# The steps of a recurrence, nine to a channel block, cut into ten (eight in the first token block)

## The chip, the cores and the metric

One core of one Trainium2 chip. Its engines work side by side, each through its own queue in order: PE (matrix products), DVE (elementwise work, scans), ACT (activation functions, copies), POOL (elementwise work), SP (here it only issues DMAs). The metric is the device time of one launch in microseconds (us); lower is better.

## The reference, cut to what matters

x is 4 sequences of 2048 tokens of 512 channels, in f32. The output is x plus two branches of its layer norm xn:

```
r, k, v = mixes of xn and the token before, times Wr, Wk, Wv        # 512 channels
per channel, from token to token (aa, bb, pp carried; decay w, bonus u):
    p  = max(pp, u + k);    e1  = exp(pp - p);      e2  = exp(u + k - p)
    y  = (e1 aa + e2 v) / (e1 bb + e2)
    p2 = max(pp + w, k);    e1b = exp(pp + w - p2); e2b = exp(k - p2)
    aa, bb, pp = e1b aa + e2b v,  e1b bb + e2b,  p2
branch 1 = (sigmoid(r) * y) Wo
hidden   = fwht(silu(xn W1) * (xn W3))                              # 2048 channels
branch 2 = hidden W2
```

The recurrence over tokens (wkv in the code) is what the change is about.

## The kernel before, in words

The tokens are worked through in eight blocks of 1024 (the loop `for i in range(n_blocks)`, i from 0), two to a sequence. Channels lie on the 128 partitions, so the 512 channels of r, k and v are four channel blocks of 128, h = 0 to 3. Each token block has these stages:

- **Projections** to r, k and v. Block 0 does them as plain products. Every later block does them as six **pairs**, n = 0 to 5 (`projected_pair`): pairs 0 and 1 give k, 2 and 3 give v, 4 and 5 give r. Pair n gives the rows of two channel blocks, h = 0 and 2 for even n, 1 and 3 for odd n. In front of the pairs stands up tile 0.
- **Up tiles**, j = 0 to 15 (`up`): the two products of the gated branch for 128 hidden channels each, gated with a tanh. 
- **Down**: the products with the two output matrices (the Hadamard transform is folded into W2 in block 0), the residual, the stores. Beside them run the token statistics, and in part the normalization, of later blocks.

A pair or an up tile is one run of `seven`, a Strassen-like scheme with seven products where eight would be plain. Its order on PE, with what other engines must have done before the next product, is this:

```
        product(pa, 0, m11, True)
        act.copy(pb, pa)
        product(pf, 4, f1, True)
        act.copy(s5, pf)
        product(pb, 5, f2, False)
        act.copy(pc, pb)
        for f in tail:
            f()
        product(pa, 1, m21, False)
        on11(pa)
        product(pb, 3, f3, False)
        act.copy(pd, pb)
        on22(pa, pb, s5)
        product(pc, 6, m22, False)
        on12(pc, s5)
        product(pd, 2, f4, False)
```

Each product adds onto a PSUM bank that ACT has just copied from another, so PE waits for such a copy, and ACT does its queue in order. f1 to f4 are differences of the right side's quarters, made by DVE. The five banks come from a ring of eight: a tile's first product takes the bank that held pb two tiles before. on11, on22 and on12 are the places where a tile's own ACT and DVE work is issued (tanh, sums with s5); `tail` is what the tile before still has to do (in an up tile: the second tanh, and three products on DVE).

**The slots.** The wkv work for a token block is a generator, and each `next` of it issues one **step**, on the queues of DVE and ACT. In up tiles a step is taken in on22 (behind the first gate, ahead of the sum onto pb) and one in on12 (behind the sum onto pc): two slots a tile. In the pairs there are three hooks a pair (on11, on22, on12), numbered 1 to 18, and a list says at which of them a step is taken: 5, 6, 8, 11, 12, 13, 14, 15, 17. The other hooks, and these too, carry the mixing of the inputs for v and r (`mix_chores`): a scaled copy on ACT, a multiply-add on DVE, then the four differences f1 to f4 on DVE. What is left of the generator after the last up tile is issued at once, by `before()`, ahead of down.

The work of one channel block, with the names that the prediction uses for its parts (tiles: sa is a0 and a1, sb is b0 and b1):

- S1: DVE scan for the running maximum into a1, and the first difference, into b1
- S2: DVE second difference, into e1
- S3: ACT two relus, of b1 into e1b and into b1
- S4: ACT two exps, of e1b and b1
- S5: ACT two relus, of e1 into k and into e1; DVE product with v and scan (aa)
- S6: ACT two exps, of k and e1; DVE scan (bb)
- S7: DVE three products and sums, to numerator part and denominator
- S8: DVE reciprocal of the first half of the denominator
- S9: DVE reciprocal of the second half; two steps of the numerator
- S10: DVE two multiply steps into r

The kernel before takes these in nine steps: S1; S3 with S2 behind it; S4; S5; S6; S7; S8; the second reciprocal; the numerator and S10. Block 0 has 4 x 9 = 36 steps and 32 slots; later blocks have 36 steps and 9 + 30 slots. For token blocks 2 to 6 the steps with the relus and with the exps of h = 1 to 3 also carry `ahead`: one and two products of the early normalization of the next block (DVE, slots in pieces_w, loaded and stored by SP).

POOL makes the differences of weights, in token blocks 0 and 1 only. SP loads the weights of an up tile or pair two tiles ahead, into a ring of three.

Down takes its right side from the up tiles and from r. It begins with four runs of ten products on quarters of the right side (the second and fourth on those with the last up tiles and with r of h = 2 and 3), while DVE makes the first differences; the fifth run of ten reads the first difference, which lies in k_sb. All of DVE's work for it is queued behind the last up tile's tail.

Of the kernel before, what the change touches and what calls it, by code (L numbers as in the profile page):

```python
# [11 lines left out]
ALU = mybir.AluOpType  # L12
# [4 lines left out]
H = 512  # L17
TB = 2 * H
# [22 lines left out]
def tile_rwkv_attn_hadamard_ffn(  # L41
# [17 lines left out]
    NB = C // P  # L59
# [7 lines left out]
    pe, dve, act, pool, sp = (InOrder(tc, e) for e in (nc.tensor, nc.vector, nc.scalar, nc.gpsimd, nc.sync))  # L67
# [24 lines left out]
    e1b, e1 = (const.tile([P, TB], F32, name=n) for n in ("e1b", "e1"))  # L92
# [11 lines left out]
    def row_of(kind, h):  # L104
        return r_of(h) if kind == 0 else (k_sb, v_sb)[kind - 1][:, h, :]
# [131 lines left out]
    def first_statistics(half):  # L237
        return token_statistics(f"f{half}", x_first[:, half * HT : (half + 1) * HT, :])

    def first_diagonals(half, rs):  # L240
        diag = v_sb[:, half, :].rearrange("p (s t q) -> p s t q", s=2, q=P)
        for t in range(HT):
            dve.tensor_scalar(diag[:, 0, t], eye_sb, rs[:, 0, t : t + 1], None, ALU.mult)
            act.activation(diag[:, 1, t], eye_sb, AF.Copy, scale=rs[:, 1, t : t + 1])
        return diag

    def first_spread(diag):
        pts = banks[6:8]
        for s in range(2):
            pe.matmul(pts[s], lhsT=ones, rhs=diag[:, s].rearrange("p t q -> p (t q)"), start=True, stop=True)  # L250
        return pts
# [43 lines left out]
    def mixed(kind):  # L295
        for b in range(NB):
            mixed_block(kind, b)


    def load_square(i, kind):  # L300
        t = half_ring({1: 0, 2: 1, 0: 0}[kind], NB, C)
        sp.dma_start(out=t, in_=wrkv[kind])
        return t
# [11 lines left out]
            act.copy(dst, pt)  # L315


    def wkv(h, ahead):

        w_h, u_h = weff[:, h : h + 1], vec[:, 4, h : h + 1]  # L320
        r, k, v = (row_of(kind, h) for kind in range(3))
        a0, a1, b0, b1 = sa[:, OFF - 1 : OFF - 1 + TB], sa[:, OFF : OFF + TB], sb[:, OFF - 1 : OFF - 1 + TB], sb[:, OFF : OFF + TB]
        first_a, first_b, last_a, last_b = a0[:, 0:1], b0[:, 0:1], a1[:, TB - 1 : TB], b1[:, TB - 1 : TB]
        tt, stt, scan, copy = dve.tensor_tensor, dve.scalar_tensor_tensor, dve.tensor_tensor_scan, dve.tensor_copy
        cy = [carry[:, h, n : n + 1] for n in range(3)]

        def below(out, t, sign):
            act.activation(out, t, AF.Relu, scale=-sign)  # L330

        def exp(t):
            act.activation(t, t, AF.Exp, scale=-1.0)

        copy(first_a, cy[0])
        scan(a1, w_h.to_broadcast([P, TB]), k, first_a, ALU.add, ALU.max)
        stt(b1, a0, w_h, k, ALU.add, ALU.subtract)
        copy(cy[0], last_a)
        yield
        below(e1b, b1, 1.0)  # L340
        below(b1, b1, -1.0)
        stt(e1, k, u_h, a0, ALU.add, ALU.subtract)
        ahead(1)
        yield
        exp(e1b)
        exp(b1)
        ahead(2)
        yield

        below(k, e1, 1.0)  # L350
        below(e1, e1, -1.0)
        copy(first_a, cy[1])
        tt(a1, b1, v, ALU.mult)
        scan(a1, e1b, a1, first_a, ALU.mult, ALU.add)
        copy(cy[1], last_a)
        yield
        exp(k)
        exp(e1)
        copy(first_b, cy[2])
        scan(b1, e1b, b1, first_b, ALU.mult, ALU.add)  # L360
        copy(cy[2], last_b)
        yield
        num, den = e1, e1b
        tt(v, k, v, ALU.mult)
        tt(den, e1, b0, ALU.mult)
        tt(den, den, k, ALU.add)
        yield
        dve.reciprocal(den[:, 0:H], den[:, 0:H])
        yield
        dve.reciprocal(den[:, H:TB], den[:, H:TB])  # L370
        yield
        tt(num, e1, a0, ALU.mult)
        tt(num, num, v, ALU.add)
        stt(r, r, 1.0, num, ALU.add, ALU.mult)
        stt(r, r, 0.5, den, ALU.mult, ALU.mult)
        yield
# [12 lines left out]
    def token_forms(eng):  # L389
        for out, x, y in ((t1, b12, b11), (t2, b22, t1), (t3, b22, b12), (t4, b21, t2)):  # L390
            eng.tensor_tensor(out, x, y, ALU.subtract)
            yield
# [59 lines left out]
    def load_parts(i, n):  # L452
        t = ring_a.tile([P, 7, KH, P], F32, tag="a", name=f"part_{i}_{n}")
        if is_first(i, n):
            sp.dma_start(out=t[:, 0:4], in_=wpart[n])
            forms_in(t)
        else:
            sp.dma_start(out=t, in_=part_w[n])
        return t
# [72 lines left out]
    def fold_products(n, m, pts=None):  # L532

        left = []
        for part in (fold[a][:, ts(k, C)] for a in range(n, m) for k in range(2)):
            pt = pts[len(left)] if pts else bank()
            pe.matmul(pt, lhsT=had_sb, rhs=part, start=True, stop=True)
            left.append((part, pt))
        return left

    def fold_evict(left):
        for part, pt in left:
            act.mul(part, pt, 0.5 / float(F) ** 0.5)
# [515 lines left out]
    for i in range(n_blocks):  # L1059
# [8 lines left out]
        def ahead(n):  # L1068
            for _ in range(n if early else 0):
                next(early, None)  # L1070


        pieces = (None for h in range(NB) for _ in wkv(h, ahead if h else lambda n: None))

        def step():
            next(pieces, None)
# [10 lines left out]
        if i == 0:  # L1087
            for kind, after in ((1, 2), (2, 0), (0, None)):
                w = w_next
                if after is not None:  # L1090
                    w_next = load_square(i, after)
                    if kind != 1:
                        mixed(after)
                if kind == 2:
                    for _ in token_forms(pool):
                        pass
                if kind == 1:
                    got = []

                    def spread_more():  # L1100
                        dve.tensor_scalar(weff, weff, -1.0, None, ALU.mult)
                        got.append(first_spread(first_diagonals(1, first_statistics(1))))

                    def fold_more():
                        got.append(fold_products(3, 4, banks[4:6]))

                    def spread_after():
                        fold_evict(got.pop(0))
                        spread_more()

                    left = first_k(0, w, spread_0, [], fold_more, lambda: None, spread_after)
                    folded_4 = fold_products(4, 5, banks[4:6])
                    left.append(lambda: fold_evict(folded_4))
                    left = first_k(1, w, got[0], left, lambda: None, lambda: None, lambda: mixed(2))
                    for f in left:
                        f()
                    turn[0] = NB
                for n in range(2 * NB if kind != 1 else 0):
                    projected(kind, w, n // 2, n % 2)
                    if kind == 2 and n == 2:  # L1120
                        fold_evict(fold_products(5, NP))
                        folded = fold_butterflies()
            parts = [load_parts(i, n) for n in order_of(i)[:2]]
        else:


            def mix_chores(*kinds):
                for kind in kinds:
                    mix_before(kind, 0)
                    for b in range(NB):  # L1130
                        if b + 1 < NB:
                            mix_before(kind, b + 1)
                        mix_here(kind, b)
                        yield
                    yield from mix_forms(kind)

            for b in range(NB):
                mix_here(1, b)
            k_forms = mix_forms(1)
            tail = up(i, 0, group(0), tail, lambda: next(k_forms))  # L1140
            for _ in k_forms:
                pass
            chores, hooks = mix_chores(2, 0), [0]
            for n in range(3 * KH):

                def hook():
                    hooks[0] += 1
                    for _ in range(1 if hooks[0] % 3 else 2):
                        next(chores, None)
                    if hooks[0] in (5, 6, 8, 11, 12, 13, 14, 15, 17):  # L1150
                        step()

                tail = projected_pair(i, n, group(1 + n), tail, hook)
# [100 lines left out]
```

## Time and profile before

| | us |
|---|---|
| median of three runs (3053.67 to 3057.03) | 3054.59 |
| profiled execution | 3052.48 |
| its span, first to last instruction | 3050.7 |
| PE busy in the span | 3014.0 |
| DVE busy | 2391.1 |
| ACT busy | 1153.9 |
| POOL busy | 213.7 |

The views used are the page (busy shares, the chain that ended last), the chain of waits in order of time (start, duration, engine, tile written), the timeline of an engine (start, duration, engine, line, operation, tiles, shape, count, and in brackets the idle time before and what ended it), and the view of stretches (length, busy time and count of PE, PEld, DVE, ACT, POOL, then the granted PE clock, DMA share, GB/s). All instructions issued through one helper have line 35, so groups are told apart by their tiles. The ends of matmuls are modelled, so the busy share of PE hides short gaps; the distance between the starts of matmuls shows them.

### The profile page before, as it was taken

What the parts mean: (1) busy time and instruction counts of PE and PEld (TensorE: products, weight loads), DVE (VectorE), ACT (ScalarE), POOL (GpSimd) and SP (SyncE); (2) the same over time, 40 slices, a digit from 0 to 9 for tenths busy, and PEclk for the clock granted to TensorE, in tenths of its full rate; (3) what the DMA queues carried; (4) which work ended last, traced back from release to release, by engine and by line L of the source; (5) the groups of instructions that cost most, each with busy time, mean ns of one, the idle gap of its engine ahead of it and who ended that gap; (6) DMA issues with size and microseconds to landing.
All of it is one profiled execution on the core that took longest, in us unless ns stands there. A gap on an engine that the chain in (4) does not pass through costs nothing.

```text
span 3050.7 us, 24995 instructions
## 1 busy us (share of the span) xinstructions
PE 3014.0 (99%) x8702; PEld 1653.5 (54%) x8702; DVE 2391.1 (78%) x2525; ACT 1153.9 (38%) x1992; POOL 213.7 (7%) x196
## 2 busy tenths in 40 slices
PE   8999999999999999999999999999999999999999
PEld 3444444447644486444854448544584445844468
DVE  7687647788878887787877878778787887877777
ACT  4334134433244333543235332443424443153421
POOL 3253012220000000000000000000000000000000
PEclk9999999999999999999999999999999999999999
DMA  4265623666422264222733236332363323622234
GB/s 174 87 209 199 220 86 128 214 215 225 141 107 102 95 228 136 105 102 85 242 122 122 98 115 218 116 121 86 139 206 105 133 86 121 203 99 73 84 128 151
DMA packets 146332, 429.14 MB, mean 141 GB/s; under 512 B 15392, under 2 KB 33824, under 8 KB 144032
## 3 DMA queue, kind: packets, MB, share of 16 engines
q1 hardware_dynamic: 145920, 426.96, 40.8%
q8 instruction: 70, 1.15, 0.2%
q10 hardware_dynamic: 288, 0.59, 0.1%
q14 instruction: 54, 0.44, 0.0%
HBM read 354.76 MB, written 72.74 MB: 140 GB/s over the span
## 4 chain that ended last, share of the span: by engine, by line
PE 95%; DVE 3%; ACT 1%; DMA 1%; issue 0%; POOL 0%; SPq 0%; DVEq 0%; ACTq 0%; POOLq 0%
PE bank L35 95%; DVE sa L35 1%; DVE e1b L35 0%; DVE right L35 0%; DMA pieces_w<-down_w 0%; DVE sb L35 0%; ACT tf L35 0%; ACT bank L35 0%; ACT e1b L35 0%; ACT sb L35 0%; DVE pieces_w L35 0%; DMA right<-w 0%; DVE v_sb L35 0%; DMA part<-wpart 0%; DVE e L35 0%
## 5 line engine op out<-in xcount | busy, mean ns | idle before, releaser
L35 PE MATMUL bank<-tf,part 128*128 128x512 f32 x2048 | 943.7, 593 | 5.0 <-ACT bank L35 5.0
L35 ACT COPY bank<-bank 128x512 f32<-128x512 f32 (+1 forms) x659 | 344.8, 523 | 1195.5 <-PE bank L35 1167.2
L35 PE MATMUL bank<-right,pieces_w 128*128 128x256 f32 (+1 forms) x2928 | 733.5, 409 | 1.6 <-DMA pieces_w<-down_w 1.6
L35 PE MATMUL bank<-xnT,part 128*128 128x512 f32 x1536 | 721.9, 592 | 0.2 <-DVE right L35 0.2
L35 PEld LDWEIGHTS bank<-tf,part 128*128 128x128 f32 x2048 | 389.3, 190 | 496.4 <-issue 456.9
L35 PEld LDWEIGHTS bank<-right,pieces_w 128*128 128x128 f32 x2928 | 556.2, 190 | 167.6 <-issue 99.3
L35 PEld LDWEIGHTS bank<-xnT,part 128*128 128x128 f32 x1536 | 291.9, 190 | 365.6 <-issue 361.9
L35 DVE SCALAR_TENSOR_TENSOR right<-right,bank 128x512 f32<-128x512 f32 x256 | 175.1, 684 | 301.7 <-ACT right L35 301.3
L35 PE MATMUL bank<-right,part 128*128 128x512 f32 x840 | 371.9, 596 | 0.0
L35 DVE TENSOR_TENSOR right<-right 128x1280 f32<-128x1280 f32 (+2 forms) x236 | 328.1, 1416 | 9.5 <-PE bank L35 8.5
L35 PEld LDWEIGHTS bank<-right,part 128*128 128x128 f32 x840 | 159.6, 191 | 205.4 <-issue 188.8
L35 ACT ACTIVATE right<-bank 128x512 f32<-128x512 f32 x308 | 184.5, 600 | 120.8 <-PE bank L35 109.9
L35 DVE RECIPROCAL e1b<-e1b 128x512 f32<-128x512 f32 x64 | 213.8, 3342 | 0.0
L35 DVE TENSOR_TENSOR right<-right,bank 128x512 f32<-128x512 f32 x256 | 173.6, 678 | 13.8 <-PE bank L35 9.4
L35 DVE TENSOR_TENSOR bank<-bank,s 128x512 f32<-128x512 f32 x256 | 167.1, 689 | 21.1 <-ACT bank L35 12.2
L35 DVE SCALAR_TENSOR_TENSOR right<-xnT,vec,right 128x1024 f32<-128x1024 f32 x92 | 121.7, 1353 | 40.6 <-ACT right L35 40.6
L35 PE MATMUL bank<-k_sb,pieces_w 128*128 128x256 f32 x630 | 146.3, 379 | 0.0
L35 PEld LDWEIGHTS bank<-k_sb,pieces_w 128*128 128x128 f32 x630 | 119.7, 190 | 16.3
L35 ACT COPY s<-bank 128x512 f32<-128x512 f32 x128 | 75.0, 586 | 136.3 <-PE bank L35 136.3
L35 PE MATMUL bank<-pieces_w,part 128*128 128x512 f32 x224 | 103.7, 601 | 15.6 <-ACT bank L35 13.3
L35 POOL TENSOR_SCALAR mean<-sums 128x8 f32<-128x8 f32 x7 | 4.8, 682 | 1568.2 <-ACT tf L35 1568.2
L35 ACT ACTIVATE right<-xnT,omm 128x1024 f32<-128x1024 f32 x92 | 100.3, 1141 | 1.9 <-PE bank L35 1.9
(120 smaller groups left out, 2350.1 us busy)
## 6 DMA issues: line engine op xcount, KB each, us to landing
part<-part_w SPq DMA_DIRECT2D x148, 896.0 KB, 4.6
pieces_w<-deep_w SPq DMA_DIRECT2D x343, 320.0 KB, 3.1
part_w<-part SPq DMA_DIRECT2D x22, 896.0 KB, 6.4
pieces_w<-down_w SPq DMA_DIRECT2D x56, 320.0 KB, 4.9
deep_w<-pieces_w SPq DMA_DIRECT2D x7, 2240.0 KB, 10.3
tf<-x SPq DMA_DIRECT2D x7, 2048.0 KB, 8.5
v_sb<-xT SPq DMA_DIRECT2D x48, 256.0 KB, 4.4
out<-v_sb SPq DMA_DIRECT2D x47, 256.0 KB, 2.2
```

The source lines that it names most:

```text
L35: return self.tc.keep_in_program_order(issue(*args, **kwargs))
```

## The change

In token blocks 1 to 7 (`ten` true) a channel block takes ten steps, S1 to S10 each on its own, and hook 9 is added to the list of hooks: ten hooks and thirty slots for forty steps. So the ten steps of a channel block take five tiles of two: S1 and S2, S3 and S4, S5 and S6, S7 and S8, S9 and S10; h = 0 takes its ten in pairs 1 to 5. In token block 0 (`ten` false) there are eight steps in four tiles: S1; S2; S3 and S4 together; S5; S6; S7; S8 with the numerator of S9; the second reciprocal with S10. Instructions are neither added nor removed.

```
-    def wkv(h, ahead):
+    def wkv(h, ahead, ten):
...
         stt(b1, a0, w_h, k, ALU.add, ALU.subtract)
         copy(cy[0], last_a)
         yield
+        stt(e1, k, u_h, a0, ALU.add, ALU.subtract)
+        yield
         below(e1b, b1, 1.0)
         below(b1, b1, -1.0)
-        stt(e1, k, u_h, a0, ALU.add, ALU.subtract)
         ahead(1)
-        yield
+        if ten:
+            yield
         exp(e1b)
         exp(b1)
         ahead(2)
...
         dve.reciprocal(den[:, 0:H], den[:, 0:H])
-        yield
-        dve.reciprocal(den[:, H:TB], den[:, H:TB])
-        yield
+        if ten:
+            yield
+            dve.reciprocal(den[:, H:TB], den[:, H:TB])
         tt(num, e1, a0, ALU.mult)
         tt(num, num, v, ALU.add)
+        yield
+        if not ten:
+            dve.reciprocal(den[:, H:TB], den[:, H:TB])
         stt(r, r, 1.0, num, ALU.add, ALU.mult)
         stt(r, r, 0.5, den, ALU.mult, ALU.mult)
         yield
...
-        pieces = (None for h in range(NB) for _ in wkv(h, ahead if h else lambda n: None))
+        pieces = (None for h in range(NB) for _ in wkv(h, ahead if h else lambda n: None, i > 0))
...
-                    if hooks[0] in (5, 6, 8, 11, 12, 13, 14, 15, 17):
+                    if hooks[0] in (5, 6, 8, 9, 11, 12, 13, 14, 15, 17):
                         step()
```

## The prediction

> **What bounds the kernel now.** I read the page first, then the chain of waits over the whole span, then the timelines of PE, ACT and DVE around each place where the chain leaves PE.
>
> ```profile
> span 3050.7 us, 24995 instructions
> ...
> PE 3014.0 (99%) x8702; PEld 1653.5 (54%) x8702; DVE 2391.1 (78%) x2525; ACT 1153.9 (38%) x1992; POOL 213.7 (7%) x196
> ...
> PE 95%; DVE 3%; ACT 1%; DMA 1%; issue 0%; POOL 0%; SPq 0%; DVEq 0%; ACTq 0%; POOLq 0%
> ```
>
> PE is the bound; DVE is at 78%. So the change, which touches no matmul, can only take or give gaps between matmuls. In the PE timeline a 512-column matmul starts every 0.43 us, a product (four of them) takes 1.72, a tile (seven products) 12.02. Where starts lie further apart, PE waited. I added these excesses up over the span: some 33 us, of which 4 in the first 20 us. The chain shows what most of the others are; here is block 3:
>
> ```profile
> 1217.24 1.29 DVE sb L35
> 1218.56 1.06 ACT e1b L35
> 1219.65 1.06 ACT sb L35
> 1220.71 0.49 ACT bank L35
> 1221.20 0.04 issue
> 1221.25 365.40 PE bank L35 x1090
> ```
>
> Read upwards: PE could run again at 1221.25 because ACT's copy of a bank ended; that copy stood behind two relus, and these waited for the difference b1 (tile sb) from DVE. The first bank copy of the pair (pf done at 1217.15 + 1.72 = 1218.87) was late by **2.38 us**. The chain shows the same five lines in blocks 2 to 7; in block 1 the timeline has it at 465.86 to 468.29 (2.43). Block 1 has it twice more in its up tiles, where POOL slows the scan (3.22 us instead of 2.35): 1.73 at 530.26 and 3.58 at 642.57, with a 0.37 just before it (a bank not read yet).
>
> A gap costs more than itself. The view of stretches, with PEclk behind the busy times:
>
> ```profile
> 1218.95:1222.36 3.41, 1.19 (x4) 0.64 (x4) 3.41 (x4) 2.73 (x4) 0.00 (x0) 1.00 0.12 50
> 1222.37:1225.77 3.40, 3.40 (x6) 1.33 (x5) 0.28 (x1) 1.07 (x2) 0.00 (x0) 0.50 0.00 0
> ...
> 846.91:850.31 3.40, 1.84 (x5) 0.88 (x6) 2.97 (x3) 2.02 (x3) 0.00 (x0) 1.00 0.00 0
> ```
>
> After a stretch of 3.41 us with PE busy 1.19, the next ran at clock 0.50 (matmuls 0.85 us apart): 1.7 us lost. After one with 1.84 busy it did not. Three such half-clock stretches follow gaps of this kind (642.1, 1222.4 and 1969.9).
>
> **The change, part by part.** Steps are named as in the section on the kernel, S1 to S10; h is the channel block.
>
> *The relus get a step of their own, a slot after the second difference.* In pair 1 (block 1 on) hook 6 now issues S2 alone, on DVE, where it stood before; ACT has nothing ahead of the bank copy, so the 2.38 go: 6 x 2.38 + 2.43 = **16.7**. Next late there would be f2 (DVE, done 1214.6) and f3 (done 1220.3, wanted 1222.3): neither is. In the up tiles S3 now always falls in the tile after S1, so b1 is long there: block 1's 1.73 + 3.58 + 0.37 = **5.7** go, and with the gaps the three half-clock stretches, 3 x 1.7 = **5.1**. Given back: 27.5.
>
> *What comes in pair 2.* There S3 (hook 8) and S4 (hook 9) both go to ACT, where before only the exps went. Before, ACT:
>
> ```profile
> 1229.25 0.58 ACT L35 COPY bank<-bank 128x512 f32<-128x512 f32 x1
> 1229.77 1.14 ACT L35 ACTIVATE right<-xnT,omm 128x1024 f32<-128x1024 f32 x1
> 1230.81 1.04 ACT L35 ACTIVATE e1b<-e1b 128x1024 f32<-128x1024 f32 x1
> 1231.76 1.04 ACT L35 ACTIVATE sb<-sb 128x1024 f32<-128x1024 f32 x1
> 1232.71 1.14 ACT L35 ACTIVATE right<-xnT,omm 128x1024 f32<-128x1024 f32 x1
> 1233.75 0.58 ACT L35 COPY bank<-bank 128x512 f32<-128x512 f32 x1
> ```
> ```profile
> 1233.43 3.60 PE L35 MATMUL bank<-pieces_w,part 128*128 128x512 f32 x8
> ```
>
> PE wants the last copy for its fifth matmul of that row, at 1233.43 + 1.72 = 1235.15; it ended at 1234.33. By the starts of such runs (1240.98, 1242.07, 1243.03, 1243.98), relus cost 1.09 and 0.96, exps 0.95 each. New order: mix 1229.77, relus 1230.81 and 1231.90, mix 1232.86, exps 1233.90 and 1234.85, copy 1235.80 to 1236.38, PE at 1236.43: **1.28 late**, in seven blocks 9.0. ACT has made it good by the next copy (the s5 copy has no PE behind it). Its ends: 0 if ACT found room, 2.38 if it cost what the old wait did. The gap leaves PE 2.1 busy in 3.41, more than the 1.84 that kept the clock.
>
> *The last step in the last tile before down.* Before, 36 steps met 39 slots and up tile 15 held none; now 40 meet 40, and it holds S9 and S10 of channel block 3: a reciprocal 3.26, two products 2.40, two into r 2.40: 8.06 of DVE, the rest of that tile unchanged. The queue behind them is the tile's tail, then down's first differences. Before:
>
> ```profile
> 1449.53 0.69 DVE L35 TENSOR_TENSOR right<-right,bank 128x512 f32<-128x512 f32 x1
> 1450.13 1.48 DVE L35 TENSOR_TENSOR k_sb<-right 128x1280 f32<-128x1280 f32 x1
> ```
> ```profile
> 1456.64 2.32 PE L35 MATMUL bank<-k_sb,pieces_w 128*128 128x256 f32 x10
> ```
>
> The difference was ready at 1451.6, PE took it at 1456.64: 5.0 of cover. DVE waited 2.6 us in that tile, which the new work fills: the tile's gated product to 1444.4, reciprocal to 1447.65, products to 1450.05, two bank sums to 1451.25, S10 to 1453.65, tail to 1455.57, difference to 1457.05. PE comes at 1457.12: **0.48 late**, in seven blocks 3.4. Its ends: 0, and 8.06 - 5.0 = 3.0 if none of the waiting is filled. The fourth product of down, which reads r, is wanted at 1454.49; r is done at 1453.7.
>
> *Block 0, eight steps in 16 tiles.* The second tile of a channel block puts S3, S4 and S5's relus on ACT: 1.09 + 0.96 + 0.95 + 0.95 + 1.12 + 0.96 = 6.03 from 133.08, so the copy ends at 139.69 and PE, due at 139.27, comes 0.47 late: four times, **1.9**. The fourth tile gives DVE 4.1 of its own and 2 x 5.7, 15.5 in 12.02. PE cares only when the tile after next takes the bank that the tail's last product reads (the 0.37 above was that). I get 0.6 of room in tile 3, 0.3 late in tile 7, 0.1 of room in tile 11, POOL's slowing counted by the rows there: **0.3**, from 0 to some 4 if all four two-input steps doubled. The four steps that were left for after block 0's last tile (312 to 325) go, but no wait of PE hung on them: the wait at 353.2 is for a transfer queued behind the statistics, and stays.
>
> *Moved at no cost.* The early normalization's products and its SP loads and stores move with S3 and S4 into up tiles 2, 7 and 12; SP's weight loads land in 4.6 us with a tile of room, and pieces_w is wanted again only at tile 15. Without that room a tile would wait up to 4.6. S9's products in pair 4 delay a DVE sum of pair 5 by 0.6, which no matmul reads. Up tiles with S9 and S10 give DVE 11.8 of 12.02; no backlog.
>
> **Sum.** 27.5 - 9.0 - 3.4 - 1.9 - 0.3 = **12.9** less. The profiled execution took 3052.48 (span and 1.8 around it): 3039.6. The runs' median, 3054.59, is 2.1 above it; if the gaps go, so does the half-clock, which I take for part of that spread, so I say **3040** for the median as well.
>
> [...] The trace has half-clock stretches after gaps of 2.4 us. [...]
>
> **Rivals.**
> - *A, pair 2 has room on ACT*: no new wait there, 3039.6 - 9.0 = 3030.6. For: a second of ACT idleness lies behind the copy; against: the copy itself is queued behind the exps. 0.12.
> - *B, the half-clock comes anyway*, from what the rows don't tell: 3039.6 + 5.1 = 3044.7. 0.08.
> - *D, the wait only moves*: pair 2 stalls as long as pair 1 did, 7 x 1.1 = 7.7, and brings two half-clock stretches, 3.4: 3050.7, no change. For: the same ACT queue, the same copy. 0.08.
> - *C, slower: the last channel block isn't done when down begins.* If DVE fills none of its waiting in tile 15, down waits 3.0 instead of 0.48: 7 x 2.5 = 17.6, and gaps of 3.0 bring a half-clock stretch in some four blocks, 6.8: 3064. It outweighs the gain from 2.3 us a block on. Against: the queue walked through above. 0.06.
>
> The forecast itself (3035 to 3043.5) has 0.66. The range 3030 to 3048 holds it with A and B. About 0.2% (6 us) is what a measurement of this kernel can tell from no change: faster 0.86, same 0.08, slower 0.06.
>
> **What would show it.** Right: no relu in the chain at the seven places; ACT's exps ahead of a bank copy in pair 2 and a PE gap of 1.3 behind; clock 1.00 throughout after the start; PE's first k_sb product of down 0.5 late, for a difference; a 0.5 gap in tiles 1, 5, 9 and 13 of block 0. Wrong: gaps over 2 us in pair 2 or at down, a gap at the start of tiles 5, 9 or 13 of block 0, or a half-clock stretch.

## The result, and the profile after

The changed kernel takes 3041.75 us (median of five runs, 3040.17 to 3044.23) against 3056.42 of the kernel before on the same chip: a ratio of 0.9953 (95% interval 0.9938 to 0.9968). The profiled execution took 3040.17, its span 3038.4. The forecast was 3040.

The page of the changed kernel:

```profile
span 3038.4 us, 25004 instructions
...
PE 3010.9 (99%) x8702; PEld 1650.6 (54%) x8702; DVE 2383.3 (78%) x2525; ACT 1152.4 (38%) x1992; POOL 215.1 (7%) x196
...
PE 89%; ACT 3%; DVE 3%; issue 0%; DVEq 0%; ACTq 0%
```

The busy shares tell nothing: 99% and 78% as before. The chain has less PE in it than before (89 for 95%) though the kernel is faster, because it counts the work that it passes through, and between waits that have shrunk to a microsecond it still goes through ACT's and DVE's whole queue. What tells is the distance between the starts of matmuls. In the execution before, PE lost 33 us in gaps of over a quarter microsecond; now 21.5. Some of that is the start, which varies; so in what follows the measure for a trace is the time from the 61st matmul (at some 38 us) to the last: **3008.4 before, 2996.8 after**, 11.5 less.

Where the gaps are now, first pair 2 of block 3 on ACT, then on PE:

```profile
1217.69 1.14 ACT L35 ACTIVATE right<-xnT,omm 128x1024 f32<-128x1024 f32 x1
1218.74 1.04 ACT L35 ACTIVATE e1b<-sb 128x1024 f32<-128x1024 f32 x1
1219.81 1.06 ACT L35 ACTIVATE sb<-sb 128x1024 f32<-128x1024 f32 x1
1220.78 1.13 ACT L35 ACTIVATE right<-xnT,omm 128x1024 f32<-128x1024 f32 x1
1221.82 1.04 ACT L35 ACTIVATE e1b<-e1b 128x1024 f32<-128x1024 f32 x1
1222.76 1.04 ACT L35 ACTIVATE sb<-sb 128x1024 f32<-128x1024 f32 x1
1223.71 0.57 ACT L35 COPY bank<-bank 128x512 f32<-128x512 f32 x1
```
```profile
1221.35 1.88 PE L35 MATMUL bank<-pieces_w,part 128*128 128x512 f32 x4
1224.34 1.98 PE L35 MATMUL bank<-pieces_w,part 128*128 128x512 f32 x4 [1.10 <-ACT bank L35]
```

Mix, two relus, mix, two exps, copy: the queue that the prediction wrote down. PE was due at 1221.35 + 1.72 = 1223.07 and came at 1224.34, 1.27 late. The relus themselves wait for nothing any more, and pair 1 has no gap.

Now the start of down in the same block, ACT and then PE:

```profile
1441.10 0.38 ACT L35 COPY bank<-bank 128x256 f32<-128x256 f32 x1
1443.58 0.69 ACT L35 ACTIVATE bank<-had_sb 128x256 f32<-128x256 f32 x2 [2.11 <-DVE right L35]
1444.21 0.33 ACT L35 COPY bank<-bank 128x256 f32<-128x256 f32 x1
```
```profile
1437.31 6.65 PE L35 MATMUL bank<-right,pieces_w 128*128 128x256 f32 x30
1444.59 2.43 PE L35 MATMUL bank<-right,pieces_w 128*128 128x256 f32 x10 [0.64 <-ACT bank L35]
```

Here the gap is not where it was forecast. Thirty matmuls of 0.216 us end at 1443.79; the fourth run of ten comes 0.80 later, and what it waits for is ACT's copy of 1444.21, which stands behind two clears (the line ahead of it), which waited 2.1 us for DVE.

### The profile page after: what moved, and what is told of

It is laid out like the page before. It is cut to its first block, busy times and chain, and to the rows that moved or that the text cites. A ratio compares the mean times of both kernels' runs of the same rounds, so it can differ in the third digit from the quotient of the medians.

```text
span 3038.4 us, 25004 instructions
## 1 busy us (share of the span) xinstructions
PE 3010.9 (99%) x8702; PEld 1650.6 (54%) x8702; DVE 2383.3 (78%) x2525; ACT 1152.4 (38%) x1992; POOL 215.1 (7%) x196
## 4 chain that ended last, share of the span: by engine, by line
PE 89%; ACT 3%; DVE 3%; issue 0%; DVEq 0%; ACTq 0%
PE bank L35 89%; DVE right L35 1%; ACT right L35 1%; DVE e1b L35 1%; ACT bank L35 1%; ACT sb L35 1%; ACT e1b L35 1%; DVE e L35 1%; DVE bank L35 0%; ACT v_sb L35 0%; ACT k_sb L35 0%; DVE v_sb L35 0%; DVEq L1255 0%; ACT e L35 0%; ACTq L35 0%
```

## The experiments

All are set against the changed kernel. In the traces I give the time from the 61st matmul to the last, which leaves the start out.

**1. The relus back behind b1.** In blocks 1 to 7 only; ten steps and hooks as changed.

```
         stt(b1, a0, w_h, k, ALU.add, ALU.subtract)
         copy(cy[0], last_a)
         yield
+        if ten: below(e1b, b1, 1.0); below(b1, b1, -1.0)
         stt(e1, k, u_h, a0, ALU.add, ALU.subtract)
         yield
-        below(e1b, b1, 1.0); below(b1, b1, -1.0)
+        if not ten: below(e1b, b1, 1.0); below(b1, b1, -1.0)
```

> Ten steps and the hooks as changed, but in token blocks 1 to 7 the relus (S3) go back into the step of the second difference (S2). Theory (the gain comes from taking the relus away from the slot behind b1): the wait of 2.4 us returns in pair 1 of seven blocks, the one of 1.28 in pair 2 goes, block 1's up tiles wait again where POOL slows the scan (1.7 to 4 us in all), and two or three half-clock stretches return (1.7 each). From 3041.75: +16.7 - 9.0 + 3 + 4.3 = 3057, between 3052 and 3060. Rival (the gain comes from ten steps and their even spread over tiles, not from the relus): no change, 3042, and no relu in the chain.

Measured: 3064.99 us (3060.61 to 3068.52); 3022.2 in the trace, 25.4 more than the changed kernel, more than the kernel before too. Pair 1 has its wait in all seven blocks (2.38, and 2.43 in block 1), pair 2 none; block 1's up tiles wait 1.99 and 3.78. The theory holds and the rival falls: ten steps without the move of the relus gain nothing. The size was missed: block 1's two waits came to 5.8, not 3, and above all the half clock came more often than in the two or three stretches expected (4.3): 25.4 - (16.7 - 9.0 + 5.8) = 11.9 us are left for it, some seven times 1.7. The mean granted clock of the profiled run was 0.996, for 1.000 in the changed kernel. The view of stretches shows one with the half clock behind it and, from the same trace, one without (534.65 to 538.05, behind the last line, ran at 1.00):

```profile
1224.14:1227.54 3.40, 1.31 (x4) 0.24 (x2) 3.40 (x5) 2.52 (x3) 0.00 (x0) 1.00 0.44 186
1227.55:1230.95 3.40, 3.28 (x4) 1.51 (x5) 1.53 (x2) 0.58 (x2) 0.00 (x0) 0.50 0.00 0
531.24:534.64 3.40, 1.58 (x5) 0.67 (x4) 2.62 (x4) 2.69 (x4) 3.40 (x2) 1.00 0.24 98
```

**2. The exps one hook later.**

```
-                    if hooks[0] in (5, 6, 8, 9, 11, 12, 13, 14, 15, 17):
+                    if hooks[0] in (5, 6, 8, 10, 11, 12, 13, 14, 15, 17):
```

> Of the ten hooks, 9 is replaced by 10, so the two exps (S4) of channel block 0 stand behind the next pair's bank copy instead of ahead of it. Theory (the 1.27 us in pair 2 are ACT's queue of mix, relus, mix, exps ahead of the copy): the gap goes in all seven blocks, and the exps at hook 10, some 1.9 us between the first output and the copy of pd, make that copy end 0.2 before PE wants it: 3041.75 - 9.0 = 3033, between 3031 and 3035. Rival (the gap is due to the relus waiting for something else, or moves on to pair 3): the time stays within 2 us of 3042, with gaps of 1 us or more in pair 2 or 3.

Measured: 3031.5 us (3031.36 to 3034.2), a ratio to the kernel before of 0.9932 (0.9917 to 0.9947); 2987.4 in the trace, 9.5 less. The gap of pair 2 is gone in all seven blocks, and none has come in pair 3:

```profile
1225.38 1.06 ACT L35 ACTIVATE e1b<-e1b 128x1024 f32<-128x1024 f32 x1
1226.34 1.05 ACT L35 ACTIVATE sb<-sb 128x1024 f32<-128x1024 f32 x1
1227.28 0.59 ACT L35 COPY bank<-bank 128x512 f32<-128x512 f32 x1
```

The exps now lie behind pair 3's first output, and the 1.9 us that they take there (1225.38 to 1227.28) hold nothing up. The cost of pair 2 was a choice of hook, not of the ten steps.

**3. The clears behind the second run of down.**

```
         d6.step(0)
-        d6.clear("f")
-        d0.clear("f")
         d6.forms(0)
         d0.step(0)
+        d6.clear("f")
+        d0.clear("f")
```

> In down, the clearing of the two f banks is issued behind the second run of ten products instead of ahead of it. Theory now (the 0.80 us at the start of down are the fourth run of ten, which adds onto a bank that ACT has still to copy, and that copy is queued behind a clear that waits for the last up tile's tail): the gap ahead of the fourth run goes, and the fifth run waits for the first difference, 0.4 late: 7 x 0.4 = 2.8 less, 3039, between 3037 and 3041. Rival (the fourth run waits for r or for the last up tile itself): the gap stays where it is, 0.8 us, and the time at 3042.

Measured: 3038.74 us (3038.36 to 3042.02); 2994.2 in the trace, 2.6 less. PE, then DVE:

```profile
1441.10 8.81 PE L35 MATMUL bank<-right,pieces_w 128*128 128x256 f32 x40
1450.17 2.40 PE L35 MATMUL bank<-k_sb,pieces_w 128*128 128x256 f32 x10 [0.26 <-issue]
```
```profile
1448.59 1.49 DVE L35 TENSOR_TENSOR k_sb<-right 128x1280 f32<-128x1280 f32 x1
```

All forty run through, so neither r nor the last up tile held the fourth run. The fifth now waits for the first difference, done at 1450.08, and starts 0.42 late. The view names no releaser for it (the 0.26 is its idle time by modelled ends); that it is the difference follows from the times, and from number 7 below, which makes the difference earlier and has no gap there. So the wait that the prediction had named at 0.48 was the second in the queue.

**4. Block 0's relus back behind b1.** Block 0 only, eight steps as changed; the mirror of experiment 1.

```
+        if not ten: below(e1b, b1, 1.0); below(b1, b1, -1.0)
         stt(e1, k, u_h, a0, ALU.add, ALU.subtract)
         yield
-        below(e1b, b1, 1.0); below(b1, b1, -1.0)
+        if ten: below(e1b, b1, 1.0); below(b1, b1, -1.0)
```

> Token block 0 alone: its relus go back into the step of the second difference, eight steps as changed. Theory: ACT's six operations ahead of a bank copy were the gap of 0.6 in tiles 1, 5, 9 and 13, so the four gaps go (2.4 us), but the transfer at some 351 us, which SP can issue only behind the statistics, lands no earlier, so PE waits up to 1.7 us there again: net 0.7 to 1 less, 3041. Rival (the wait at 351 went because DVE no longer holds work over into down, which let POOL and SP go sooner): the four gaps go and no wait comes back: 2.4 less, 3039.4.

Measured: 3056.23 us (3053.34 to 3060.83), 3012.0 in the trace: 15 more, and as slow as the kernel before (ratio 1.0012, 1.0002 to 1.0021). Both theories missed it. The four gaps of 0.6 did go, but three waits of 2.97, 3.36 and 5.00 came, in tiles 4, 8 and 12. ACT's line for the first:

```profile
175.16 1.06 ACT L35 ACTIVATE e1b<-sb 128x1024 f32<-128x1024 f32 x1 [6.24 <-DVE sb L35]
```

The fourth tile of a channel block (15.5 us of DVE in 12.02) does leave DVE late, by some 3 us at the start of the next to go by the first wait. With the relus a tile behind b1 nobody waits for that; with the relus beside it ACT does, and PE behind ACT. The profiled run's mean granted clock was 0.998, for 1.000 in the changed kernel; the kernel before, with three half-clock stretches, has 0.998 too. At the place of the wait at 351 PE came some 15 us later than in the changed kernel and still waited, 0.26: the transfer had moved along with it, so it does not land at a fixed time.

**5. Block 0's six operations as four and four.**

```
-        below(k, e1, 1.0); below(e1, e1, -1.0)
+        if ten: below(k, e1, 1.0); below(e1, e1, -1.0)
         copy(first_a, cy[1])
...
+        if not ten: below(k, e1, 1.0); below(e1, e1, -1.0)
         exp(k)
         exp(e1)
```

> Token block 0 alone: the two relus of S5 go from S5's step to S6's, so ACT has four operations (some 4 us) ahead of the bank copy in the second and in the third tile of a channel block, not six and two; everything else as changed. Theory (six operations on ACT are the 0.6): the gaps in tiles 1, 5, 9 and 13 go, 2.4 us. For the wait at 351, two theories. A, the transfer lands at a fixed time and block 0's delay merely hid the wait: PE waits there again, 1.7 to 2.4, net 0 to 0.7 less, 3041 to 3042. B, the chain of statistics, POOL and SP ahead of it follows PE and became shorter when DVE's leftover work went: no wait there, 2.4 less, 3039.4.

Measured: 3041.75 us (3038.81 to 3041.91), which tells little beside the spread at the start (below); 2995.0 in the trace, 1.9 less. The four gaps are gone (2.4), and at 354 PE waits 0.55 for the transfer: between A and B, nearer to B. What the chain ahead of that transfer did is seen on POOL. Kernel before, then the changed one:

```profile
327.24 0.92 POOL L35 TENSOR_SCALAR mean<-sums 128x8 f32<-128x8 f32 x1 [51.52 <-ACT tf L35]
```
```profile
328.89 0.24 POOL L35 TENSOR_SCALAR mean<-sums 128x8 f32<-128x8 f32 x1 [49.52 <-ACT tf L35]
```

The same tiny operation took 0.92 us while DVE ran down's first differences late, behind the four leftover steps, and 0.24 when these were done. Experiment 6, which has the leftover steps, has 0.92 again; this one 0.24. The second piece is the store of the statistics behind it, which the next load waits for. From the chain, before and in this experiment:

```profile
336.28 2.51 DMA stat_d<-rs
```
```profile
338.09 1.54 DMA stat_d<-rs
```

Counted from one and the same matmul in each kernel (the one that starts at 316.30 before), the POOL operation starts after 10.9 us everywhere. The transfer that PE waits for is issued after 24.6 before and 24.3 in experiment 6, and after 22.8 to 22.9 in all kernels without leftover steps: the chain follows PE, as theory B has it.

**6. The move of the relus alone, in the kernel before.** Nine steps, old hooks.

```
-        below(e1b, b1, 1.0); below(b1, b1, -1.0)
         stt(e1, k, u_h, a0, ALU.add, ALU.subtract)
-        ahead(1)
         yield
+        below(e1b, b1, 1.0); below(b1, b1, -1.0)
+        ahead(1)
         exp(e1b)
```

> The kernel before with one part of the change alone, in all blocks: nine steps, old hooks, but the relus (S3) leave the step of S2 and join that of the exps (S4). Theory (moving the relus is the gain, the ten steps are not): pair 1's waits and block 1's go, pair 2 keeps 1.3 (the same ACT operations stand ahead of its copy), the start of down has no gap of 0.8, but channel blocks whose S3 and S4 share a tile with S5 put six operations on ACT, 0.6 each, two in each of eight blocks (9 us), and block 0's wait at 351 returns (1.7): 3041.75 - 5.6 + 8 + 1.7 - 1.2 = 3045, between 3041 and 3049. Rival (the ten steps carry the gain): 3050 or more, with gaps over 2 us in pair 1 or in block 1's up tiles.

Measured: 3043.1 us (3042.59 to 3046.49), ratio 0.9964 (0.9951 to 0.9976); 2998.9 in the trace, 2.1 more than the changed kernel. Pair 1's waits and block 1's of 1.73 and 3.58 are gone, pair 2 has its 1.27 (1.36 in block 1), each later block has 0.43 and 0.49 in two up tiles where six operations meet, down starts without a gap, and the wait at 351 is back with 1.81. So most of the gain is this one move (9.4 of the 11.5 us in the trace). In blocks 1 to 7 the ten steps only trade two half-microsecond gaps a block for one of 0.8; block 0's eight steps take away the wait at 351, for four gaps of 0.6 where nine steps have two.

**7 and 8. What the experiments point to.** Number 7 joins 2 and 3 and issues the first difference of down ahead of up tile 12; number 8 adds 5.

```
-        d6.forms(0)
...
+            if i and j == 12:
+                y11 = parts_of(0, 0)
+                difference(k_flat[:, 0 : QR * H // 2].rearrange("p (q t) -> p q t", q=QR), y11[1], y11[0])
             if j == NF - 1:
                 for u in range(7):
```

> The changed kernel with hook 10 in place of 9, the clears of the f banks behind the second run of down, and the first difference of down issued ahead of up tile 12 (blocks 1 to 7). Theory: the gaps of pair 2 (9.0 us) and both waits at the start of down (0.8, of which 0.42 was left by the clears alone) go, and tile 12 takes 1.4 us of DVE without a gap: 3031.5 with hook 10 alone, less 5.6: 3026, between 3024 and 3029. Rival (the difference only moves DVE's lateness to something else at the start of down): a gap of 0.4 or more per block stays there, 3029 to 3032.

> As the one before, and block 0's relus of S5 moved to S6's step. By theory A for the wait at 351: 3026 less 0 to 0.7. By theory B: 3026 - 2.4 = 3023.6. Against the kernel before (3052.8 on the last chip) a ratio of 0.990 to 0.991.

Measured: 3026.76 us (3025.21 to 3029.0), ratio 0.9913 (0.9898 to 0.9927), and **3024.25 us** (3022.93 to 3025.53), ratio 0.9904 (0.9889 to 0.9918); in the traces 2981.2 and 2978.3. The waits of PE in number 8, all of them:

```profile
PE bank L35 <- DMA right<-w: 7.8, 1, 7.8
PE bank L35 <- DVE tf L35: 2.8, 1, 2.8
```

Both are in the first 21 us. Number 7's start of down has no gap left. For the wait at 351, number 7 has 0.26 and number 8 none, where theory A had 1.7 or more come back with number 8: A falls.

## Why the prediction was right

The three largest terms were right because the waits were read from the trace and the new queue on ACT was laid out instruction by instruction. That the sum came so close is in part luck: the start of down cost 2.2 us more than forecast, the wait at 351 gave 1.7 that the sum did not have, and the two nearly cancel. Point by point, with what the trace after has (gaps by the starts of matmuls, in us):

| term | forecast | measured |
|---|---|---|
| pair 1, seven blocks | -16.7 | -16.7 |
| block 1's up tiles | -5.7 | -5.7 |
| half-clock stretches | -5.1 | -4.6 |
| pair 2, seven blocks | +9.0 | +9.0 (6 x 1.27 + 1.36) |
| start of down, seven blocks | +3.4 | +5.6 (7 x 0.80) |
| block 0, second tiles | +1.9 | +2.4 (0.63 + 3 x 0.58) |
| block 0, fourth tiles | +0.3 | 0 |
| wait at 351 | 0 | -1.7 |
| sum | -12.9 | -11.7 |

From the first to the last matmul the traces differ by 11.4 and the spans by 12.3; the first matmul came 0.9 earlier, ahead of anything that the change touches. Without that the profiled execution would have taken 3041.1, not 3040.17, for the forecast 3039.6. The 3040 for the median took part of the spread of the runs for half-clock stretches. The spread did shrink, from 7.6 to 4.1 us, but the median still lies 1.6 above the profiled execution, whose clock was full.

- *The relus* were the cause, and the move is the gain: experiment 1 shows it from one side, 6 from the other.
- *Pair 2* was right in mechanism and size; experiment 2 shows the queue to be the cause. Rival A is out, since ACT had no room there, and D, since the new wait is half the old and brought no half clock.
- *The start of down* failed. The step said that the fourth run was safe since r was done in time. It had checked what the run reads, not the bank that it adds onto: that had to be copied first, and the copy's place in ACT's queue is behind a clear that waits for the last up tile's tail. Experiment 3 shows it. The term was 0.80 a block for 0.48.
- *Rival C*, the slower one, was the same place with a larger price: it needed 2.3 a block, and the queue gave 0.8.
- *Block 0, second tiles*: right in mechanism (experiment 5), 0.58 to 0.63 for 0.47. The six operations took the 6.03 us of the forecast (132.36 to 138.39 in tile 1); PE then started 0.15 behind the end of the copy, where the step had taken 0.06.
- *Block 0, fourth tiles*: the overload is there, as experiment 4 shows, but no bank was wanted before DVE had read it. The 0.3 was within what the estimate can't tell.
- *The wait at 351* "stays", said the prediction, since no wait of PE hung on the four leftover steps. It looked for a wait on DVE; the steps worked through POOL, whose operation took 0.92 us in the kernels with them and 0.24 in those without, and SP, which issues the transfer behind it. Counted from the same matmul, the weights' transfer was issued 1.66 earlier after the change: 0.69 of it is POOL's operation, 0.96 the store of the statistics (2.51 us before, some 1.55 after). Why that store is slower beside the leftover steps stays open, as does why the transfer still lands 0 to 0.55 late in the kernels without them.
- *The half clock* is gone from the profiled execution, as forecast (mean granted clock 1.000, for 0.998 before), and so rival B is out. That it can follow a gap of 2.4 us, the trace of experiment 1 shows again: PE was busy 1.31 of the 3.40 us at 1224.14, and the next 3.40 ran at clock 0.50.

## What to carry to other kernels

When a chain of steps is spread over tiles, ask of each engine's queue what is issued between a step and the bank copy that PE wants next; an operation that must wait for another engine belongs a slot after its input, and one that merely takes time belongs where that queue has its idle time, which need not be the next slot. When checking that a matmul is not late, check the bank that it adds onto as well as what it reads, and follow the queue ahead of that copy. Gaps of PE that look small in a busy share of 99% can cost more than themselves: in the kernel before, gaps of 3.58, 2.38 and 2.38 us were each followed by 3.41 us at clock 0.50, which cost another 1.5 to 1.7 us each.

## What the runs showed of the hardware

- **Three stretches at half clock.** In the trace of the kernel before, the granted clock behind the start was 1.00 but for three stretches of 3.41 us at 0.50. They begin at 642.10, 1222.36 and 1969.88, which is 580.27 and 747.52 us apart, 170 and 219 times 3.4133. In the 3.41 us ahead of them PE was busy 0.46, 1.19 and 1.39 us (as the view has it, with modelled ends). Cut at the same distances, the rest of that trace has its least busy stretches at 1.42, 1.67 and 1.84 us (464.60, 2713.99 and 846.90), and the clock behind each of these stayed at 1.00. The one with 1.42 and the one with 1.39:

```profile
464.60:468.01 3.41, 1.42 (x4) 0.35 (x2) 3.41 (x5) 2.42 (x3) 0.97 (x2) 1.00 0.97 364
1966.47:1969.88 3.41, 1.39 (x3) 0.68 (x4) 3.41 (x3) 2.45 (x4) 0.00 (x0) 1.00 0.04 15
```

  So waits of one length did not all cost the same. Of the seven in pair 1 there (six of 2.38 us, one of 2.43), two were followed by such a stretch, some 1.7 us more, and five were not; nor were those of 1.73 and 1.74 (530.26 and 353.23).
- **The start varies by more than some edits bring.** In the profiled execution of experiment 3 the eight matmuls from 19.62 us on took 6.74 us, for 3.70 in those of the kernel before and the changed one. Its run, at a mean granted clock of 0.999, took 3042.0; the other three, at 1.000, took 3038.4 to 3038.8. The medians, of 4 to 10 runs, carry this; the time from the 61st matmul on does not.
